# Layer 2's sums of bases in two parts, and copies from DRAM to DRAM beside layer 1's edges

## The chip, the cores and the metric

The kernel runs on one core of one Trainium2 chip. The metric is the device time of one execution in microseconds; a comparison uses the medians of several executions. A core has five engines that matter here: TensorE (PE), VectorE (DVE), ScalarE (ACT), GpSimd (POOL) and SyncE (SP), which only issues transfers. Each works its own instructions in order, and semaphores tie them together.

## What is computed

The reference is two graph layers of one kind, a mixture of experts, four graph layers of another kind and a quantized feed-forward part, each added to a running x of 10000 rows of 512. Only the first piece matters here:

```python
def rgcn_gate_layer(x, row, col, edge_type, basis, att, gate_w, root, bias):
    w = jnp.einsum('rb,bio->rio', att, basis)          # 2 relations, 30 bases of 512 x 512
    x_j = x[col]                                       # 5000 edges
    msgs = []
    for r in range(NUM_RELATIONS):
        gate = jax.nn.sigmoid(x_j @ gate_w[r, :, 0])
        msgs.append(gate[:, None] * x_j @ w[r])
    msg = jnp.where((edge_type == 0)[:, None], msgs[0], msgs[1])
    agg = jax.ops.segment_sum(msg, row, num_segments=x.shape[0])
    return agg + x @ root + bias
...
h = jax.nn.relu(rgcn_gate_layer(x, ..., basis1, att1, ...))
out = rgcn_gate_layer(h, ..., basis2, att2, ...)
...
x = x + _L0_gnn_ref(_layernorm(x, axis=-1), ...)
```

So each of the two layers needs two weighted sums of 30 matrices (one for each relation), a product for every node (`x @ root`), and a gated product for every edge that is added to the row of its target.

## The kernel before

The work runs in stages: the sorting of the edges, the node pass of layer 1, the edges of layer 1, the edges of layer 2, and then the rest (the node product of layer 2, the experts, the other graph layers). DRAM tensors link them: `xn_d` holds the normalized rows, `r1_d` layer 1's sums, and `a2_d` the rows to which layer 2's edges are added.

*Node pass* (`rgcn_nodes1`). It goes over 20 blocks of up to 512 rows. A block is loaded into `x_in`, stored unchanged into `a2_d`, normalized into `xn` and stored into `xn_d`, turned by PE, multiplied with `root` (L742), copied by ACT to `o_nodes` (L746), given the bias by POOL (L748) and stored into `r1_d`. The blocks' loads and stores are all on SP's queue (`rows_to`, L139).

*Sums of bases* (`relation_weights`). For each of 30 bases SP loads 1 MB into one of the two buffers of the pool `stream`, and DVE adds it into the weights of both relations (L635 for the first basis, L637 for the others). A sum works on 128x2048 numbers.

*Edges* (`rgcn_edges`). There are RT = 41 tiles of 128 sorted edges. A tile is gathered from DRAM by POOL (`fetch`, L614). In `make_ready` DVE takes its two dot products with the gate vectors (L669), ACT the sigmoid (L674), DVE the mask of the relation (L675); PE turns the keys (L680), and DVE makes `same` (L682), a matrix that adds up edges with the same target. In `add_up` PE multiplies by it (L689) and ACT copies the result to `aT` (L693). In `put` PE multiplies by the weights (L703), ACT copies to `o` (L708), and POOL adds the rows to DRAM with a scatter (`scatter_add`, L619). The loop runs over i: tile i is fetched, tile i-3 made ready, tile i-5 added up, tile i-6 put. On PE, POOL, ACT and DVE the order of this loop is the one written (`manual_schedule`); everything outside it, and all of SP's queue, is put in order by a scheduler, which lets later work fill the gaps that it sees.

*Placing* (`place_nodes`). A generator of some sixty small steps, which the edges' loops carry beside them: `take(i)` says in which iterations a step is taken. Ten of the steps are `equal_keys`, in which PE turns four columns of keys into a PSUM pool of two buffers and DVE compares each (L211, L212).

In the program's order, layer 1's sums stand behind the node pass; layer 2's sums stand between the two loops of edges, but DVE may take them earlier.

Of the kernel before, what the change touches and what calls it, by code (L numbers as in the profile page):

```python
# [8 lines left out]
F32 = mybir.dt.float32  # L9
# [4 lines left out]
OP = mybir.AluOpType  # L14
# [3 lines left out]
P = 128  # L18
N = 10000
D = 512  # L20
KC = D // P
E = 5000
ET = 40
# [19 lines left out]
CAP = 625  # L43
CT = (CAP + P - 1) // P
LAYERS = 4
FETCHED, READY = 6, 3
LN_EPS = 1e-5
BN_EPS = 1e-5
# [21 lines left out]
def gnn_ffn_kernel(ctx: ExitStack, tc: tile.TileContext, I, out, dram):  # L70
# [62 lines left out]
    def rows_to(sb, d, b, store=False):  # L133

        for n, a0, a1 in block_parts(b):
            r0 = (b * 4 + a0) * P
            v = d[r0 : r0 + n * (a1 - a0), :].rearrange("(a p) d -> p a d", p=n)
            s = sb[:n, a0:a1, :]
            nc.sync.dma_start(v, s) if store else nc.sync.dma_start(s, v)  # L139

    def row_broadcast(pool, d, width, name):

        t = pool.tile([P, width], F32, name=name)
        nc.sync.dma_start(t, bass.AP(tensor=d.tensor, offset=d.offset, ap=[[0, P], [1, width]]))
        return t
# [467 lines left out]
    def gather(dst, src, idx):  # L613
        return nc.gpsimd.indirect_dma_start(  # L614
            out=dst, out_offset=None, in_=src, in_offset=bass.IndirectOffsetOnAxis(ap=idx, axis=0)
        )
# [6 lines left out]


    def relation_weights(basis, att_d, pool, stream, tag):
        att = row_broadcast(pool, att_d, RELATIONS * BASES, f"att_{tag}")
        ws = pool.tile([P, RELATIONS, KC * D], F32, name=f"w_{tag}")
        for b in range(BASES):
            t = stream.tile([P, KC, D], F32, name="basis")
            nc.sync.dma_start(t, basis[b].rearrange("(k p) o -> p k o", p=P))  # L630
            tf = t.rearrange("p k o -> p (k o)")
            for r in range(RELATIONS):
                c = att[:, r * BASES + b : r * BASES + b + 1]
                if b == 0:
                    nc.vector.tensor_scalar(ws[:, r], tf, c, None, op0=OP.mult)  # L635
                else:
                    nc.vector.scalar_tensor_tensor(ws[:, r], tf, c, ws[:, r], op0=OP.mult, op1=OP.add)  # L637
        return ws

    def rgcn_edges(tag, meta, src_d, relu, ws, gate_d, dst_d, beside, take):  # L640

        with ExitStack() as s:
            fix = s.enter_context(tc.tile_pool(name=f"re_fix_{tag}", bufs=1))
            wk = s.enter_context(tc.tile_pool(name=f"re_wk_{tag}", bufs=3))
            pk = s.enter_context(tc.tile_pool(name=f"re_pk_{tag}", bufs=1, space=PSUM))
            pa = s.enter_context(tc.tile_pool(name=f"re_pa_{tag}", bufs=2, space=PSUM))
            po = s.enter_context(tc.tile_pool(name=f"re_po_{tag}", bufs=2, space=PSUM))
            gate = row_broadcast(fix, gate_d, RELATIONS * D, "gate")  # L650
            of_rel = fix.tile([P, RT, RELATIONS], F32, name="of_rel")
            nc.vector.tensor_scalar(of_rel[:, :, 0], meta["attr"], 0.0, None, op0=OP.is_equal)
            nc.vector.tensor_scalar(of_rel[:, :, 1], meta["attr"], 0.0, None, op0=OP.not_equal)
            w_all = ws.rearrange("p r w -> p (r w)")

            got, ready, sums = {}, {}, {}

            def fetch(t):
                got[t] = wk.tile([P, D], F32, name="x", bufs=FETCHED + 2)
                gather(got[t], src_d, meta["gidx"][:, t : t + 1])  # L660

            def make_ready(t):
                x, kt = got[t], meta["key"][:, t : t + 1]
                if relu:
                    nc.scalar.activation(x, x, AF.Relu)
                dots = wk.tile([P, RELATIONS], F32, name="dots")
                prod = wk.tile([P, D], F32, name="prod", bufs=2)
                for r in range(RELATIONS):
                    nc.vector.scalar_tensor_tensor(  # L669
                        prod, x, 1.0, gate[:, r * D : (r + 1) * D], op0=OP.mult, op1=OP.mult,  # L670
                        accum_out=dots[:, r : r + 1],
                    )
                g = wk.tile([P, RELATIONS + 1], F32, name="g")
                nc.scalar.activation(g[:, :RELATIONS], dots, AF.Sigmoid)  # L674
                nc.vector.scalar_tensor_tensor(  # L675
                    dots, g[:, :RELATIONS], 1.0, of_rel[:, t, :], op0=OP.mult, op1=OP.mult,
                    accum_out=g[:, RELATIONS:],
                )
                ps_k = pk.tile([P, P], F32, name="ps_k")
                nc.tensor.transpose(ps_k, kt.to_broadcast([P, P]), ident)  # L680
                same = wk.tile([P, P], F32, name="same", bufs=4)
                nc.vector.tensor_scalar(same, ps_k, kt, g[:, RELATIONS:], op0=OP.is_equal, op1=OP.mult)  # L682
                ready[t] = same

            def add_up(t):
                x, same = got.pop(t), ready.pop(t)
                ps_a = pa.tile([P, KC, P], F32, name="ps_a")
                for k in range(KC):
                    nc.tensor.matmul(  # L689
                        ps_a[:, k, :], lhsT=x[:, k * P : (k + 1) * P], rhs=same, start=True, stop=True  # L690
                    )
                sums[t] = wk.tile([P, KC, P], F32, name="aT")
                nc.scalar.copy(sums[t], ps_a)  # L693

            def put(t):
                aT = sums.pop(t)
                w0 = nc.values_load(
                    meta["w_at"][:, t : t + 1], engines=(mybir.EngineType.PE,), min_val=0, max_val=KC * D,
                    skip_runtime_bounds_check_because="it is 0 or KC * D by the comparison that makes it",
                )  # L700
                ps_o = po.tile([P, D], F32, name="ps_o")
                for k in range(KC):
                    nc.tensor.matmul(  # L703
                        ps_o, lhsT=aT[:, k, :], rhs=w_all[:, bass.ds(w0 + k * D, D)],
                        start=k == 0, stop=k == KC - 1,
                    )
                o = wk.tile([P, D], F32, name="o")
                nc.scalar.copy(o, ps_o)  # L708
                scatter_add(dst_d, meta["sidx"][:, t : t + 1], o)

            E_ = mybir.EngineType
            with tc.manual_schedule(engines={E_.PE, E_.Pool, E_.Activation, E_.DVE}):
                for i in range(RT + FETCHED):
                    if i < RT:
                        fetch(i)
                    if i >= FETCHED - 1 and i - FETCHED + 1 < RT:
                        add_up(i - FETCHED + 1)
                    if i >= FETCHED:
                        put(i - FETCHED)
                    if READY <= i < RT + READY:  # L720
                        make_ready(i - READY)
                    if take(i):
                        next(beside, None)

    def rgcn_nodes1(root, bias, pools):


        ld, tp, small, pt, po = pools
        for b in range(NB):
            tiles, parts, cols = block_tiles(b), block_parts(b), block_cols(b)  # L730
            x = ld.tile([P, 4, D], F32, name="x_in")
            rows_to(x, I["x"], b)
            rows_to(x, a2_d, b, store=True)
            xn = ld.tile([P, 4, D], F32, name="xn")
            layernorm(small, xn, x, tiles, parts, on_act=True)
            rows_to(xn, xn_d, b, store=True)
# [15 lines left out]

    with ExitStack() as s:
        wpool = s.enter_context(tc.tile_pool(name="w_rel", bufs=1))
        stream = s.enter_context(tc.tile_pool(name="stream", bufs=2))
        src_meta = s.enter_context(tc.tile_pool(name="src_meta", bufs=1))
        wk = s.enter_context(tc.tile_pool(name="sort", bufs=1))
        place_wk = s.enter_context(tc.tile_pool(name="place_wk", bufs=1))
# [1 line left out]
        with ExitStack() as n:  # L760
# [18 lines left out]
                meta_pool,  # L779
            )  # L780
            rgcn_nodes1(root, bias, (ld, tp, small, pt, po))
            ws = relation_weights(I["L0_gnn_basis1"], I["L0_gnn_att1"], wpool, stream, "1")
        placing = place_nodes(by_dst, place_wk, ps, meta_pool)
        rgcn_edges(
            "1", by_src, xn_d, False, ws, I["L0_gnn_gate_w1"], r1_d, placing,
            lambda i: i >= FETCHED and i % 2 == 0,
        )
        ws = relation_weights(I["L0_gnn_basis2"], I["L0_gnn_att2"], wpool, stream, "2")
        rgcn_edges("2", by_src, r1_d, True, ws, I["L0_gnn_gate_w2"], a2_d, placing, lambda i: True)
        for _ in placing:  # L790
            pass

# [753 lines left out]
    with ExitStack() as n:  # L1546
# [36 lines left out]
        def fetch(t):  # L1583
            if t < NT:
                n_ = rows_of(t // 4, t % 4)
                old[t] = wk.tile([P, D], F32, name="x_old", bufs=3)
                gather(old[t][:n_], x2_d, node_at[:n_, t : t + 1])
# [233 lines left out]
```

## Time and profile before

| | us |
|---|---|
| median of 3 runs | 4662.56 (4658.36 to 4666.1) |
| the profiled execution | 4666.98 |
| its span | 4665.2 |
| first gather of layer 1's edges | at 532.50 |
| first and last scatter of layer 1's edges | at 565.51 and 839.71 |
| first gather of layer 2's edges | at 845.12 |
| layer 2's sums on DVE | 408.6 to 628 |

Times inside the profile count from the start of the span. A line of a group gives the line of the kernel, the engine, the operation, its output and inputs, and how often it ran. A line of the order of time gives the start, the duration, the engine and the operation, and in brackets how long the engine had been idle before it and what released it. The releaser is inferred from semaphores, and where several were waited for, only one is named.

### The profile page before, as it was taken

What the parts mean: (1) busy time and instruction counts of PE and PEld (TensorE: products, weight loads), DVE (VectorE), ACT (ScalarE), POOL (GpSimd) and SP (SyncE); (2) the same over time, 40 slices, a digit from 0 to 9 for tenths busy, and PEclk for the clock granted to TensorE, in tenths of its full rate; (3) what the DMA queues carried; (4) which work ended last, traced back from release to release, by engine and by line L of the source; (5) the groups of instructions that cost most, each with busy time, mean ns of one, the idle gap of its engine ahead of it and who ended that gap; (6) DMA issues with size and microseconds to landing.
All of it is one profiled execution on the core that took longest, in us unless ns stands there. A gap on an engine that the chain in (4) does not pass through costs nothing.

```text
span 4665.2 us, 42798 instructions
## 1 busy us (share of the span) xinstructions
PE 4046.1 (87%) x13624; PEld 2048.0 (44%) x13624; DVE 2820.7 (60%) x5906; ACT 1679.5 (36%) x2992; POOL 1569.0 (34%) x1127
## 2 busy tenths in 40 slices
PE   6799568897999945968887999999999999999997
PEld 3443234443444422434443555545555455544443
DVE  7887865554545465646755546644575455755776
ACT  4334112232333310116423523354233532334775
POOL 3434334441000036865542113311142111422443
PEclk9899789898988866989889999999999999999998
DMA  8677654457555414986411123102231012311332
GB/s 276 228 260 258 216 123 88 86 105 184 192 171 182 146 48 84 162 164 218 153 54 43 73 77 119 42 17 81 85 108 37 27 75 104 90 30 46 110 109 98
DMA packets 293120, 556.20 MB, mean 119 GB/s; under 512 B 41216, under 2 KB 71969, under 8 KB 291871
## 3 DMA queue, kind: packets, MB, share of 16 engines
q1 hardware_dynamic: 219632, 364.67, 23.2%
q0 software_dynamic: 73264, 188.79, 17.8%
q8 instruction: 111, 1.82, 0.2%
q14 instruction: 113, 0.93, 0.1%
HBM read 292.40 MB, written 260.95 MB: 119 GB/s over the span
## 4 chain that ended last, share of the span: by engine, by line
PE 38%; DVE 8%; DMA 4%; ACT 3%; issue 2%; POOL 1%; POOLq 0%; DVEq 0%; ACTq 0%
PE ps_b L1317 15%; PE ps_d L1317 8%; PE ps_o L1593 5%; PE ps_e L1317 4%; PE ps_x L1424 2%; DMA x<-xg_d,gpos 2%; PE ps_x L1248 2%; ACT feat L1413 1%; DMA x_in<-x_d,node_at 1%; DVE stats L1402 1%; DVE x L1234 1%; DVE feat L1252 1%; PE ps_q L1661 1%; DVE feat L1332 1%; DVE t L1340 0%
## 5 line engine op out<-in xcount | busy, mean ns | idle before, releaser
L1317 PE MATMUL ps_b<-feat,w 128*128 128x512 f32 (+1 forms) x1120 | 499.7, 587 | 25.6 <-ACT feat L1413 25.5
L1317 PE MATMUL ps_d<-feat,w_s 128*128 128x512 f32 (+1 forms) x1120 | 503.6, 586 | 4.3 <-issue 3.1
L1325 ACT ACTIVATE feat<-ps_b,cols 128x512 f32<-128x512 f32 (+1 forms) x300 | 203.8, 683 | 568.1 <-PE ps_b L1317 555.4
L1352 POOL TENSOR_TENSOR feat<-feat 128x1024 f32<-128x1024 f32 (+1 forms) x70 | 162.5, 2322 | 623.2 <-DVE feat L1351 598.2
L1365 POOL TENSOR_TENSOR feat<-feat,p 128x1024 f32<-128x1024 f32 (+1 forms) x70 | 176.3, 2519 | 483.0 <-ACT feat L1325 474.2
L637 DVE SCALAR_TENSOR_TENSOR w<-basis,att,w 128x2048 f32<-128x2048 f32 x116 | 315.8, 2731 | 15.6 <-DMA basis<-in_L_gnn_basis 15.6
L742 PE MATMUL ps_o<-root,xT 128*128 128x512 f32 (+1 forms) x632 | 323.6, 625 | 0.0
L1317 PEld LDWEIGHTS ps_b<-feat,w 128*128 128x128 f32 x1120 | 208.4, 191 | 255.5 <-issue 209.4
L703 PE MATMUL ps_o<-w,aT 128*128 x656 | 304.6, 609 | 0.1
L1426 DVE TENSOR_TENSOR x_rows<-ps_x,be 128x512 f32<-128x512 f32 (+1 forms) x237 | 157.4, 685 | 231.0 <-PE ps_x L1424 231.0
L1317 PEld LDWEIGHTS ps_d<-feat,w_s 128*128 128x128 f32 x1120 | 203.3, 192 | 202.2 <-issue 183.0
L918 PE MATMUL ps_n<-root,rT 128*128 128x512 f32 (+1 forms) x632 | 288.6, 613 | 0.0
L1317 PE MATMUL ps_b<-t,w_s 128*128 128x512 f32 (+1 forms) x560 | 259.2, 603 | 21.7 <-ACT feat L1325 21.6
L1317 PE MATMUL ps_e<-feat,w 128*128 128x512 f32 (+1 forms) x560 | 264.9, 614 | 12.9 <-DVE feat L1283 12.9
L614 POOL DMA_INDIRECT x<-xg_d,gpos x160 | 175.0, 1093 | 287.8 <-issue 71.8
L1317 PE MATMUL ps_b<-feat,w_s 128*128 128x512 f32 (+1 forms) x560 | 253.7, 591 | 0.0
L1413 ACT ACTIVATE feat<-feat,bn_sm 128x512 f32<-128x512 f32 (+2 forms) x320 | 236.6, 809 | 3.4 <-DVE bn_sm L1532 3.4
L1234 DVE SCALAR_TENSOR_TENSOR x<-we,srt_d,x 128x512 f32<-128x512 f32 x160 | 139.9, 889 | 156.6 <-DMA x<-xg_d,gpos 149.5
L1402 DVE BATCH_NORM_STATS2 stats<-feat 128x6 f32<-128x512 f32 (+1 forms) x320 | 202.7, 667 | 46.7 <-POOL feat L1365 33.1
L1248 PE MATMUL ps_x<-same,x 128*128 128x128 f32 x1280 | 176.9, 287 | 58.6 <-DVE same L1244 24.1
L1248 PEld LDWEIGHTS ps_x<-same,x 128*128 128x128 f32 x1280 | 167.9, 199 | 126.9 <-issue 42.2
L1237 ACT ACTIVATE x<-x 128x512 f32<-128x512 f32 x160 | 99.3, 628 | 295.2 <-DVE x L1234 179.3
(483 smaller groups left out, 7656.1 us busy)
## 6 DMA issues: line engine op xcount, KB each, us to landing
basis<-in_L_gnn_basis SPq DMA_DIRECT2D x60, 1024.0 KB
xg_d<-x_rows SPq DMA_DIRECT2D x234, 256.0 KB
xg_d<-x_in SPq DMA_DIRECT2D x39, 512.0 KB
x_in<-in_x SPq DMA_DIRECT2D x19, 1024.0 KB
a_d<-x_in SPq DMA_DIRECT2D x19, 1024.0 KB
xn_d<-xn SPq DMA_DIRECT2D x19, 1024.0 KB
r_d<-o_nodes SPq DMA_DIRECT2D x19, 1024.0 KB
r_in<-r_d SPq DMA_DIRECT2D x19, 1024.0 KB
```

The costliest lines, as they stand in the source:

```text
L637: nc.vector.scalar_tensor_tensor(ws[:, r], tf, c, ws[:, r], op0=OP.mult, op1=OP.add)
L703: nc.tensor.matmul(ps_o, lhsT=aT[:, k, :], rhs=w_all[:, bass.ds(w0 + k * D, D)], start=k == 0, stop=k == KC - 1,)
L742: nc.tensor.matmul(ps_o[:n], lhsT=xT[:, k, a * P : a * P + n], rhs=root[:, k, :], start=k == 0, stop=k == KC - 1,)
L918: nc.tensor.matmul(ps_o[:n_], lhsT=rT[:, k, a * P : a * P + n_], rhs=root[:, k, :], start=k == 0, stop=k == KC - 1,)
L1234: nc.vector.scalar_tensor_tensor(x, we, by_dst["attr"][:, t : t + 1], x, op0=OP.mult, op1=OP.add)
L1248: nc.tensor.matmul(ps_a[:, k, :], lhsT=x[:, k * P : (k + 1) * P], rhs=same, start=True, stop=True)
L1317: nc.tensor.matmul(ps[fo], lhsT=A[a][:, k, fo * P : (fo + 1) * P], rhs=x[:, k, :], start=first and k == 0, stop=k == 1, skip_group_check=True,
L1325: nc.scalar.activation(dst[:, fo, :], ps[fo], func, bias=b, scale=scale)
L1365: nc.gpsimd.tensor_tensor(b22, b22, p5, OP.add)
L1402: nc.vector.bn_stats(stats[:, k, 2 * p + j, :], big[:, k, s0 + j * w : s0 + (j + 1) * w])
L1413: nc.scalar.activation(hb, hb, AF.Relu, bias=sm[:, fo, 3:4], scale=sm[:, fo, 2:3])
L1593: nc.tensor.matmul(ps_o[:n_], lhsT=big[:, kc, t * P : t * P + n_], rhs=W2[kc], start=kc == 0, stop=kc == KC - 1,)
```

## The change

Four things change.

1. `relation_weights` no longer runs its sums at once. It returns the weights' tile and a generator that adds one basis at each step. Layer 1's are all taken at once, as before. Of layer 2's, eight (`EARLY_BASES`) are taken inside the node stage, behind layer 1's; the other 22 are taken one by one inside layer 1's loop of edges, at i = 4, 6, ... 46, on DVE behind `make_ready`.
2. Placing steps in layer 1's loop are taken at odd i from 7 on; before it was even i from 6 on. In layer 2's loop each iteration takes one, as before.
3. The node pass no longer stores its rows into `a2_d`. Instead, in each of the first 40 iterations of layer 1's loop, SP issues a copy of 250 rows from the input x to `a2_d`, from DRAM to DRAM. The copy of iteration i waits until that iteration's gather has landed.
4. The pool `stream` has three buffers instead of two.

```diff
+EARLY_BASES = 8
...
     def relation_weights(basis, att_d, pool, stream, tag):
...
-        for b in range(BASES):
...
-        return ws
+        def sums():
+            for b in range(BASES):
+                t = stream.tile([P, KC, D], F32, name="basis")
+                nc.sync.dma_start(t, basis[b].rearrange("(k p) o -> p k o", p=P))
+                tf = t.rearrange("p k o -> p (k o)")
+                for r in range(RELATIONS):
+                    c = att[:, r * BASES + b : r * BASES + b + 1]
+                    if b == 0:
+                        nc.vector.tensor_scalar(ws[:, r], tf, c, None, op0=OP.mult)
+                    else:
+                        nc.vector.scalar_tensor_tensor(ws[:, r], tf, c, ws[:, r], op0=OP.mult, op1=OP.add)
+                yield
+
+        return ws, sums()
...
                     if i < RT:
-                        fetch(i)
+                        fetched = fetch(i)
...
-                    if take(i):
-                        next(beside, None)
+                    beside(i, fetched)
...
             rows_to(x, I["x"], b)
-            rows_to(x, a2_d, b, store=True)
...
-        stream = s.enter_context(tc.tile_pool(name="stream", bufs=2))
+        stream = s.enter_context(tc.tile_pool(name="stream", bufs=3))
...
             rgcn_nodes1(root, bias, (ld, tp, small, pt, po))
-            ws = relation_weights(I["L0_gnn_basis1"], I["L0_gnn_att1"], wpool, stream, "1")
+            ws1, adding = relation_weights(I["L0_gnn_basis1"], I["L0_gnn_att1"], wpool, stream, "1")
+            for _ in adding:
+                pass
+            ws2, adding = relation_weights(I["L0_gnn_basis2"], I["L0_gnn_att2"], wpool, stream, "2")
+            for _ in range(EARLY_BASES):
+                next(adding)
         placing = place_nodes(by_dst, place_wk, ps, meta_pool)
+
+        def beside_1(i, ready):
+            if i >= 4 and i % 2 == 0:
+                next(adding, None)
+            elif i > FETCHED:
+                next(placing, None)
+            if i < ET:
+
+                c0, c1 = N * i // ET, N * (i + 1) // ET
+                cp = nc.sync.dma_start(a2_d[c0:c1, :], I["x"][c0:c1, :])
+                tc.add_manual_dep(
+                    cp.ins, ready.ins.name,
+                    mybir.DependencyInfo(mybir.DependencyClass.Sync, mybir.DependencyReason.DATA),
+                    reason="not all at once, and not beside the nodes",
+                )
+
+        rgcn_edges("1", by_src, xn_d, False, ws1, I["L0_gnn_gate_w1"], r1_d, beside_1)
+        for _ in adding:
+            pass
         rgcn_edges(
-            "1", by_src, xn_d, False, ws, I["L0_gnn_gate_w1"], r1_d, placing,
-            lambda i: i >= FETCHED and i % 2 == 0,
+            "2", by_src, r1_d, True, ws2, I["L0_gnn_gate_w2"], a2_d, lambda i, _: next(placing, None)
         )
-        ws = relation_weights(I["L0_gnn_basis2"], I["L0_gnn_att2"], wpool, stream, "2")
-        rgcn_edges("2", by_src, r1_d, True, ws, I["L0_gnn_gate_w2"], a2_d, placing, lambda i: True)
```

More of the change, by code (lines that the diff above doesn't have):

```diff
@@ L627, in relation_weights, with rgcn_edges @@
         ws = pool.tile([P, RELATIONS, KC * D], F32, name=f"w_{tag}")
-        for b in range(BASES):
[L629 to L637, printed above, removed]
-        return ws
-    def rgcn_edges(tag, meta, src_d, relu, ws, gate_d, dst_d, beside, take):
+        def sums():
[11 more added lines that the diff above has]
+        return ws, sums()
+    def rgcn_edges(tag, meta, src_d, relu, ws, gate_d, dst_d, beside):
         with ExitStack() as s:
@@ L659, in fetch @@
                 got[t] = wk.tile([P, D], F32, name="x", bufs=FETCHED + 2)
-                gather(got[t], src_d, meta["gidx"][:, t : t + 1])
+                return gather(got[t], src_d, meta["gidx"][:, t : t + 1])
             def make_ready(t):
```

## The prediction

> **What bounds the kernel now.** I read the page first (span, engine shares, groups), then the busy time by stage, then POOL's and SP's order of time where the stage of the change begins, then DVE's order of time inside it, and last the DMA view of two windows.
>
> ```profile
> span 4665.2 us, 42798 instructions
> ...
> L637 DVE SCALAR_TENSOR_TENSOR w<-basis,att,w 128x2048 f32<-128x2048 f32 x116 | 315.8, 2731 | 15.6 <-DMA basis<-in_L_gnn_basis 15.6
> ```
>
> A sum takes 2.73 us on average, 2.34 in the median; a basis has two.
>
> ```profile
> 250.00:500.00 250.00, 238.82 (x745) 100.53 (x745) 204.12 (x388) 100.24 (x213) 106.68 (x52) 0.98 0.72 246
> 500.00:640.00 140.00, 53.52 (x163) 28.16 (x163) 118.31 (x135) 12.68 (x28) 43.26 (x22) 0.68 0.66 198
> 640.00:800.00 160.00, 137.01 (x519) 75.83 (x518) 74.73 (x309) 35.68 (x84) 74.83 (x56) 0.98 0.52 92
> ```
>
> Columns: stretch, its length, busy time of PE, PE loads, DVE, ACT, POOL, clock, DMA share, GB/s. The node pass (to 500) has PE busy 238.8 of 250 us. From 500 to 640 PE idles, 53.5 of 140, and DVE is full, 118.3: that is the hole. After 640 PE is the fullest again and DVE is under half.
>
> ```profile
> 504.88 12.51 SPq L630 DMA_DIRECT2D basis<-in_L_gnn_basis  x3
> ...
> 522.18 1.21 SPq L139 DMA_DIRECT2D r_d<-o_nodes  x2
> ```
> ```profile
> 507.14 7.70 POOL L748 TENSOR_TENSOR o_nodes<-o_nodes,bias 128x1024 f32<-128x1024 f32 x2 [4.43 <-ACT o_nodes L746]
> 532.50 3.14 POOL L614 DMA_INDIRECT x<-xn_d,gidx_s  x1 [17.66 <-DVE w L637]
> ...
> 565.51 2.00 POOL L619 DMA_INDIRECT r_d<-o,sidx  x1 [20.74 <-ACT o L708]
> 567.82 2.24 POOL L614 DMA_INDIRECT x<-xn_d,gidx_s  x1 [0.30 <-issue]
> 572.38 3.51 POOL L619 DMA_INDIRECT r_d<-o,sidx  x1 [2.32 <-DVE dots L675]
> ...
> 834.20 1.55 POOL L619 DMA_INDIRECT r_d<-o,sidx  x1 [3.93 <-issue]
> 839.71 1.55 POOL L619 DMA_INDIRECT r_d<-o,sidx  x1 [3.95 <-DMA r_d<-o,sidx]
> 845.12 1.01 POOL L614 DMA_INDIRECT x<-r_d,gidx_s  x1 [3.86 <-DMA r_d<-o,sidx]
> ```
>
> Three things to see. POOL ends the last bias add at 514.84, but SP issues the last node stores at 522.18 to 523.39, because loads of bases that wait for DVE stand ahead of them; the first gather goes out at 532.50. (Its named releaser is a sum of DVE; the last stores landing fits too, and since both go in the change I need not choose.) The scatters run from 565.51 to 839.71: 40 intervals, 6.86 us each; the first five take 72.4 us, the other 35 take 5.77 each. And at the end, with nothing else to wait for, each scatter still waits 3.95 us for the one before to land: 1.55 + 3.95 = 5.50 us a tile is the floor of this chain.
>
> ```profile
> 642.23 0.16 DVE L675 SCALAR_TENSOR_TENSOR dots<-g,of_rel 128x2 f32<-128x2 f32 x1 [2.41 <-ACT g L674]
> ...
> 649.18 0.16 DVE L675 SCALAR_TENSOR_TENSOR dots<-g,of_rel 128x2 f32<-128x2 f32 x1 [3.25 <-ACT g L674]
> ```
> ```profile
> q0 software_dynamic: 2434, 5.69, 55.2%
> ```
> ```profile
> q1 hardware_dynamic: 5469, 10.87, 58.4%
> ```
>
> DVE idles 2.41 + 3.25 = 5.66 us in each pair of tiles (11.39 us). The two queue lines are of 640 to 700 (gathers and scatters alone) and of 560 to 620 (bases too): packets, MB, share of 16 engines.
>
> **The change, part by part.** The sum is against the profiled execution, 4666.98 us (span 4665.2 and 1.8 around it), 4.4 above the median 4662.56.
>
> *Before the first gather.* Today 15 of layer 2's bases are summed by 541, the eighth at about 488; then DVE goes on without a pause, and SP's loads wait for it. With only eight ahead, DVE is quiet from about 488 and SP's stores wait for nobody. ACT's last copy to o_nodes ends at 510.5; a bias add on 16 rows should need about 1.3 us when no sum runs beside it (3.3 now), so the stores go out at about 512, and land in 6 us (9.1 now, with bases in flight): first gather at 518, 14 us earlier. Bounds: 0 (another releaser) to 17.
>
> *From gather to first scatter.* Today 33.0 us. The first gather's issue falls from 3.14 us (a sum beside it) to about 1, and the sums of 541 to 565 that stand between the DVE steps fall away but for one basis at i=4, 4.7 us. First product 6.5 us after the gather, `same` 3.3 later, matmuls, copies and the one basis 10.5: 20 us, so the first scatter is at 538.
>
> *The 40 intervals.* Three floors, all near each other:
> (a) PE and DVE. Two sums (4.7 us) now stand on DVE after `same` of each even i; the next `same` comes 7.1 us later (0.32 + 4.62 + two products 1.31 + sigmoid and masks 0.85) instead of 4.43. In odd i stand the placing steps, whose third transpose on PE waits for DVE's first `eq`: the whole delay of 2.7 us lands on PE. A pair costs 11.39 + 2.7 = 14.1 us in the ten `equal_keys` steps; the nine pairs behind them, 11.6 today, get about 13.2, the first one 10.4: 270 us, 6.75 a tile.
> (b) The scatter chain: 1.59 of issue, some 0.4 for issues beside a sum (3.51 at 572.38 against 1.55), and the landing. That is 3.95 alone and at most 4.87 with bases in flight (567.51 to 572.38); with 4.6, 6.6 a tile.
> (c) DMA. From the queue lines: gathers and scatters take 0.552 x 60 us for 10.5 tiles, 3.14 us a tile; a basis 0.584 x 60 us for 10.4 MB-sized loads, 3.38, half of one a tile 1.69. A copy of 250 rows (0.51 MB) is the unknown. At a load's rate it is 1.65 us: 6.5 a tile. If reading and writing DRAM cost a pass each, 3.3: 8.1.
>
> [...] I take 6.5 to 7.2, nearest to the row, since each copy is released by a gather landing, about when the scatter before it has landed, so part of it lies in the gap in which POOL issues.
>
> Three floors at 6.5 to 7.2 don't overlap perfectly: 7.15 a tile, 286 us, last scatter at 824 against 839.7: 16 us earlier.
>
> *Moved past queues.* SP issues 40 copies of about 0.4 us each, 16 us over 290. A copy that waits for a gather holds up the basis loads behind it; with three buffers, a load has about five tiles of lead over its sum, so nothing waits. If that cover were gone, each of 19 loads would show up to 3.4 us on DVE. POOL gets no new instruction.
>
> *Costed at nothing.* The a2 stores and their 21 waits on SP leave the node pass (20.5 MB, 61 us of all engines at a load's rate): PE, 95% busy from 250 to 500, covers it; the bounds are -10 (the 15 us wait for `key_s` before 206 shrinks) to +5 (another order of instructions). The last basis is summed at i=46, when layer 2's first product still waits for gathers; the last copy belongs to i=39, some 40 us ahead of the first scatter into a2_d. Layer 2 itself keeps its length: one placing step more, in a loop that has slots to spare.
>
> Sum: 4667.0 - 16 = 4651, or 4646.6 by the median; I say 4646.
>
> **The rivals.**
> *Slower: DMA becomes the bound.* [...] It decides from (839.7 - 538) / 40 = 7.54 us a tile. For it: the floor is 6.5 even at the kindest price, and layer 1's gathers and scatters alone hold 55% of the engines. Against: with bases in flight a landing stayed under 4.9.
> *Faster by more.* PE's waits for `eq` don't add up because PE has caught up elsewhere, and the copies fit in the gaps: 6.3 a tile, last scatter at 790, 50 us earlier: 4613. For it: the chain's own floor is 5.5, and DVE has 5.66 us idle a pair for 4.7 of sums. Against: floor (c).
> *Nothing to see.* The earlier start is worth 14 + 13 us (first gather, and 20 us instead of 33 to the first scatter). At 7.5 us a tile, 40 x (7.5 - 6.86) = 26 us of it are given back: 4662, within 9. That the change does not do what it says (the scheduler floating sums up into the gaps again) belongs here; inside the hand-written order, though, DVE keeps the written place.
>
> **How the numbers follow.** Forecast 0.5 (4625 to 4660, a fifth of it within 0.2%, some 9 us, which is about what a measurement of this kernel can tell), slower rival 0.25, faster one 0.15, nothing 0.10. Faster 0.4 + 0.15 = 0.55; same 0.1 + 0.1 = 0.20; slower 0.25. The range runs from 4608 to 4692: it leaves out about half of each outer rival.
>
> **What would show it.** First gather near 518, and no sum between 490 and that; first scatter near 538; scatters 7 us apart, last one near 824; odd tiles longer than even ones by 5 us or more, with PE waiting on `eq`; landing after a scatter's issue 4.6 us. DMA share in that stage near 0.9. I am wrong if scatters stand over 7.5 us apart, if POOL's waits there name the scatter before, or if the node pass ends more than 10 us away from 510.

## The result and the profile after

The changed kernel is slower: 4672.16 us (median of 14 runs, 4661.32 to 4690.96) against 4656.73 for the kernel before (14 runs beside it), a ratio of 1.0033 with an interval of 1.0022 to 1.0043. The forecast was 4646 and faster.

The two profiled executions are nearly equal, 4667.41 us after and 4666.98 before; the one of before lies 10 us above the median of its runs, the one of after 5 us below. So the spans say nothing here, and I read the marks of the stage instead (a tile is the distance from the first to the last scatter, divided by 40):

| us from the start of the span | before | forecast | after |
|---|---|---|---|
| first gather | 532.50 | 518 | 517.18 |
| first scatter | 565.51 | 538 | 534.09 |
| a tile (40 intervals) | 6.86 | 7.15 | 7.97 |
| last scatter | 839.71 | 824 | 852.70 |
| first gather of layer 2 | 845.12 | – | 858.06 |
| last scatter of layer 2 | 1094.61 | – | 1102.82 |

Layer 1's edges begin 31.4 us earlier and end 13.0 later. The medians differ by 15.4.

From the page of the changed kernel, its span and the group of the sums:

```profile
span 4665.6 us, 42847 instructions
...
L641 DVE SCALAR_TENSOR_TENSOR w<-basis,att,w 128x2048 f32<-128x2048 f32 x116 | 291.3, 2527 | 14.4 <-DMA basis<-in_L_gnn_basis 14.4
```

The sums became cheaper by themselves, 291.3 us against 315.8 for the same 116. Their own length is not what costs. The busy time by stage (stretch, length, PE, PE loads, DVE, ACT, POOL, clock, DMA share, GB/s):

```profile
250.00:500.00 250.00, 236.47 (x757) 101.10 (x756) 160.57 (x396) 96.88 (x207) 89.03 (x51) 0.97 0.55 186
500.00:640.00 140.00, 96.69 (x316) 53.50 (x316) 80.57 (x195) 24.32 (x55) 60.52 (x38) 0.83 0.66 188
640.00:800.00 160.00, 111.79 (x361) 62.16 (x361) 96.77 (x227) 25.93 (x59) 60.12 (x41) 0.82 0.72 193
450.00:500.00 50.00, 49.42 (x148) 22.30 (x147) 4.61 (x27) 16.96 (x34) 16.22 (x9) 1.00 0.39 120
```

The hole of 500 to 640 is half filled, PE 96.7 us against 53.5. But the stage behind it, which was good before, has become like it: PE 111.8 of 160 instead of 137.0, at a clock of 0.82 instead of 0.98. No engine is full there, and DMA is busy for 72%. The last row shows what I had not expected: DVE works 4.61 us in the 50 us ahead of the hole. The eight bases were done at 398.

POOL's order of time:

```profile
513.27 1.25 POOL L751 TENSOR_TENSOR o_nodes<-o_nodes,bias 16x512 f32<-16x512 f32 x1 [1.13 <-ACT o_nodes L749]
517.18 1.01 POOL L615 DMA_INDIRECT x<-xn_d,gidx_s  x1 [2.65 <-issue]
...
534.09 1.64 POOL L620 DMA_INDIRECT r_d<-o,sidx  x1 [8.07 <-ACT o L714]
...
637.36 1.58 POOL L620 DMA_INDIRECT r_d<-o,sidx  x1 [2.92 <-DVE prod L675]
...
647.21 1.58 POOL L620 DMA_INDIRECT r_d<-o,sidx  x1 [6.97 <-ACT g L680]
...
652.94 1.58 POOL L620 DMA_INDIRECT r_d<-o,sidx  x1 [2.06 <-DVE prod L675]
...
838.69 4.15 POOL L620 DMA_INDIRECT r_d<-o,sidx  x1 [4.14 <-DMA r_d<-o,sidx]
846.78 1.90 POOL L620 DMA_INDIRECT r_d<-o,sidx  x1 [3.94 <-issue]
852.70 1.55 POOL L620 DMA_INDIRECT r_d<-o,sidx  x1 [4.02 <-DMA r_d<-o,sidx]
858.06 1.01 POOL L615 DMA_INDIRECT x<-r_d,gidx_s  x1 [3.80 <-DMA r_d<-o,sidx]
```

The bias add takes 1.25 us and the gather follows at 517.18: the start went as forecast. A long and a short interval make a pair: 9.85 and 5.73 us here, 15.6 in all, where 14.1 was forecast (and a difference of 5 or more, for 4.1 here). The issue of 4.15 us at 838.69 is a scatter beside a sum. Inside the long interval, in PE's order of time with one sum of DVE:

```profile
638.52 0.95 PE L212 MATMUL ps_s<-ident,key_d 128*128 128x128 f32 x2 [3.92 <-DVE eq L213]
...
639.26 1.91 PE L695 MATMUL ps_a<-same,x 128*128 128x128 f32 x8
...
640.97 5.29 PE L709 MATMUL ps_o<-w,aT 128*128 x8
...
646.21 1.06 PE L695 MATMUL ps_a<-same,x 128*128 128x128 f32 x8
...
647.10 3.60 PE L709 MATMUL ps_o<-w,aT 128*128 x8
...
647.67 4.61 DVE L641 SCALAR_TENSOR_TENSOR w<-basis,att,w 128x2048 f32<-128x2048 f32 x2
...
655.00 0.95 PE L212 MATMUL ps_s<-ident,key_d 128*128 128x128 f32 x2 [3.98 <-DVE eq L213]
```

PE waits 3.92 us for `eq`, which stands on DVE behind the sums. Then the same eight products that take 1.06 us in the next tile take 1.91, and the eight behind them 5.29 instead of 3.60: another 2.5 us. This is the clock, as the busy time of these two tiles shows (the granted clock is the third number from the end):

```profile
639.26:646.21 6.95, 6.95 (x19) 3.88 (x18) 1.81 (x8) 0.58 (x1) 0.98 (x1) 0.63 0.99 299
646.21:650.65 4.44, 4.44 (x20) 2.47 (x19) 3.48 (x5) 1.27 (x3) 3.14 (x2) 1.00 0.67 141
```

It repeats behind each of the ten waits: there the first eight products take 1.91 or 1.92 us, and the granted clock over both groups is 0.61 to 0.79, against 1.00 in the tiles between.

The waits in the stage from 530 to 850 (engine, output, line, what it waited for: us in all, times, longest), and the two DMA queues from 640 to 700 (packets, MB, share of 16 engines):

```profile
PE ps_s L212 <- DVE eq L213: 46.5, 10, 7.7
...
PE ps_s L458 <- DVE tot_f L456: 14.7, 1, 14.7
...
DVE w L641 <- DMA basis<-in_L_gnn_basis: 14.4, 6, 5.6
```
```profile
q1 hardware_dynamic: 2353, 7.81, 41.4%
q0 software_dynamic: 1709, 3.96, 31.4%
```

The ten `equal_keys` steps wait 46.5 us; the placing steps behind them have long single waits. Gathers and scatters take 31.4% of the engines instead of 55.2%, in part because fewer tiles pass (3.96 MB instead of 5.69).

### The profile page after: what moved, and what is told of

It reads as the page before. It is cut to its first block, busy times and chain, and to the rows that moved or that the text cites. A ratio compares the mean times of both kernels' runs of the same rounds, so it can differ in the third digit from the quotient of the medians.

```text
span 4665.6 us, 42847 instructions
## 1 busy us (share of the span) xinstructions
PE 4065.5 (87%) x13624; PEld 2062.4 (44%) x13624; DVE 2809.1 (60%) x5906; ACT 1681.2 (36%) x2992; POOL 1555.4 (33%) x1127
## 4 chain that ended last, share of the span: by engine, by line
PE 37%; DVE 9%; DMA 4%; ACT 3%; issue 2%; POOL 1%; DVEq 0%; POOLq 0%; ACTq 0%
PE ps_b L1341 14%; PE ps_d L1341 8%; PE ps_o L1617 5%; PE ps_e L1341 4%; PE ps_x L1448 2%; DMA x<-xg_d,gpos 2%; PE ps_x L1272 2%; DVE stats L1426 1%; ACT feat L1437 1%; DMA x_in<-x_d,node_at 1%; DVE feat L1276 1%; DVE x L1258 1%; PE ps_q L1685 1%; DVE feat L1356 1%; DVE t L1364 1%
## 5 line engine op out<-in xcount | busy, mean ns | idle before, releaser
L641 DVE SCALAR_TENSOR_TENSOR w<-basis,att,w 128x2048 f32<-128x2048 f32 x116 | 291.3, 2527 | 14.4 <-DMA basis<-in_L_gnn_basis 14.4
```

## The experiments

Medians; the ratio is to the kernel before, run beside each. First and last scatter come from the profiled execution, and "a tile" is their distance over 40. Executions of these kernels spread by 12 to 48 us, so a single profile tells where time is spent, and the ratio what it is worth.

| run | us | ratio | first, last scatter | a tile |
|---|---|---|---|---|
| after | 4672.16 | 1.0033 [1.0022, 1.0043] | 534.1, 852.7 | 7.97 |
| e1 placing, then sums | 4674.94 | 1.0052 [1.0035, 1.0069] | 536.3, 852.3 | 7.90 |
| e2 no copies | 4666.31 | 1.0021 [1.0008, 1.0034] | 537.8, 841.2 | 7.59 |
| e3 copies alone | 4685.66 | 1.0070 [1.0049, 1.0090] | 579.3, 847.4 | 6.70 |
| e4 all 30 ahead | 4634.79 | 0.9957 [0.9942, 0.9972] | 573.2, 833.3 | 6.50 |
| e5 e1 without copies | 4653.55 | 1.0006 [0.9997, 1.0016] | 544.2, 839.9 | 7.39 |
| e6 e5, 20 ahead | 4628.01 | 0.9950 [0.9934, 0.9967] | 574.8, 819.4 | 6.11 |
| e7 30 ahead, no copies | 4657.98 | 1.0017 [1.0006, 1.0028] | 618.2, 847.9 | 5.74 |
| e8 e1 without loads | 4617.9 (one run) | – | 530.5, 811.1 | 7.02 |
| e9 20 ahead | 4647.8 | 0.9969 [0.9957, 0.9981] | 540.8, 825.2 | 7.11 |
| e10 halves | 4665.96 | 1.0011 [0.9997, 1.0025] | 531.6, 838.8 | 7.68 |
| e11 halves, no copies | 4631.11 | 0.9942 [0.9928, 0.9956] | 546.1, 816.6 | 6.76 |
| e12 e10, older gather | 4654.69 | 0.9987 [0.9974, 0.9999] | 543.3, 861.1 | 7.94 |
| e13 e11, 14 ahead | 4641.76 | 0.9962 [0.9953, 0.9972] | 567.4, 821.1 | 6.34 |
| e14 e12, four buffers for o | 4643.21 | 0.9982 [0.9971, 0.9993] | 538.5, 832.6 | 7.35 |

### Sums or copies: each alone, and the order on DVE (e1 to e4)

e1 takes the placing step in even iterations, ahead of the sums, so that `eq` no longer stands behind them:

```diff
         def beside_1(i, ready):
+            if i >= FETCHED and i % 2 == 0:
+                next(placing, None)
             if i >= 4 and i % 2 == 0:
                 next(adding, None)
-            elif i > FETCHED:
-                next(placing, None)
```

> In layer 1's loop the placing step and the two sums both stand in the even iterations, the placing step first. The work and the transfers are those of the changed kernel. If PE's wait for eq behind the two sums (3.98 us at 655.00) and the slow matmuls after it are the cost (theory A), a pair of tiles falls from 16.0 to about 12 us, the last scatter comes near 534 + 40 x 6.1 = 778, and the kernel takes about 4600. If the transfers beside the loop cost it (B), or DVE's plain load (C), the pair stays at 15 to 16 us and the time within 10 us of the changed kernel's 4672.

PE's wait for `eq` fell, but nothing was gained: 7.90 a tile. Its waits from 530 to 850, then SP's and DVE's order of time:

```profile
DVE w L641 <- DMA basis<-in_L_gnn_basis: 67.4, 14, 7.1
...
PE ps_k L686 <- DVE same L688: 48.3, 13, 8.4
...
PE ps_s L212 <- DVE eq L213: 17.8, 15, 2.1
```
```profile
613.54 8.75 SPq L801 DMA_DIRECT2D a_d<-in_x  x2
622.38 0.53 SPq L634 DMA_DIRECT2D basis<-in_L_gnn_basis  x1
...
631.03 4.61 DVE L641 SCALAR_TENSOR_TENSOR w<-basis,att,w 128x2048 f32<-128x2048 f32 x2 [6.70 <-DMA basis<-in_L_gnn_basis]
```

Two copies hold SP's queue from 613.54 to 622.29, while they wait for their gathers; the load of a basis behind them goes out at 622.38, and DVE, whose sum needs it, waits 6.70 us and starts at 631.03. Nothing else runs on DVE in these 6.70 us. So a second bound stood right behind the first.

e2 leaves out the copies and stores the rows in the node pass again (`rows_to(x, a2_d, b, store=True)`, as before):

```diff
+            rows_to(x, a2_d, b, store=True)
...
-            if i < ET:
...
-                cp = nc.sync.dma_start(a2_d[c0:c1, :], I["x"][c0:c1, :])
...
```

> The sums as in the changed kernel, but no copies from DRAM to DRAM: the rows are stored into a2_d in the node pass as before. A: pairs still 15.5 to 16 us, last scatter 850, the time of the changed kernel within 10 us. B: with 20 MB less beside the loop, pairs fall to 14 or less, last scatter before 820, at least 30 us faster than the changed kernel.

Still slower than before. PE's order of time is that of the changed kernel:

```profile
653.37 0.95 PE L212 MATMUL ps_s<-ident,key_d 128*128 128x128 f32 x2 [3.93 <-DVE eq L213]
...
654.11 1.91 PE L695 MATMUL ps_a<-same,x 128*128 128x128 f32 x8
```

So, in these two profiled executions, the sums alone, as this change places them, make 7.59 of the 7.97 us, and the copies the last 0.38.

e3 is the kernel before with the copies in place of the a2 stores; the text of the sums stays as it was:

```diff
                     if i < RT:
-                        fetch(i)
+                        fetched = fetch(i)
...
+                    if tag == "1" and i < ET:
+                        c0, c1 = N * i // ET, N * (i + 1) // ET
+                        cp = nc.sync.dma_start(a2_d[c0:c1, :], I["x"][c0:c1, :])
...
-            rows_to(x, a2_d, b, store=True)
```

> The kernel before, with the copies from DRAM to DRAM beside layer 1's edges in place of the stores in the node pass; sums and placing as before. A: scatters beyond the hole stay 5.8 to 6.3 us apart (the copies cost at most 0.5 a tile), the kernel is within 15 us of the one before. B: 7 us apart or more, 40 us slower than before.

The dearest of all, but not by the copies alone: the sums went elsewhere. SP's and DVE's order of time:

```profile
557.63 241.03 SPq L726 DMA_DIRECT2D a_d<-in_x  x40
...
857.46 9.13 DVE L637 SCALAR_TENSOR_TENSOR w<-basis,att,w 128x2048 f32<-128x2048 f32 x4
```

The 40 copies, which wait for their gathers, hold SP's queue from 557.63 to 798.66, and the loads of the last six bases stand behind them. So no sum runs between 569 and 830, and a tile still takes 6.70 us, against 5.77 in the kernel before behind its first five intervals. The last six bases are added from 830.70 on, most of them among layer 2's first tiles: its first scatter comes 38.7 us after its first gather instead of 20.3, and its edges take 264 us against 249. So this run does not give the price of the copies by itself; e7 below does.

e4 is the changed kernel with no sum in the loop:

```diff
-EARLY_BASES = 8
+EARLY_BASES = 30
```

> EARLY_BASES = 30: all of layer 2's sums ahead of layer 1's edges, none among them; copies and odd placing steps as in the changed kernel. DVE sits idle from 398 to about 523 in the changed kernel, 22 bases of 4.7 us need 103. A and C: scatters 5.8 to 6.2 us apart from the first on, the first one at 534 to 550, the last near 780, and the time 60 to 75 us under the changed kernel's, so also under the one before: 4600 to 4610. B: the copies still hold the loop at 7 us a tile or more, last scatter past 815.

Faster than before, with 6.50 a tile. The first gather went out at 538.11, and its issue took 19 us where the next takes 0.96:

```profile
512.32 43.92 DVE L641 SCALAR_TENSOR_TENSOR w<-basis,att,w 128x2048 f32<-128x2048 f32 x18
...
538.11 19.01 POOL L615 DMA_INDIRECT x<-xn_d,gidx_s  x1 [17.96 <-DMA r_d<-o_nodes]
557.43 0.96 POOL L615 DMA_INDIRECT x<-xn_d,gidx_s  x1 [0.30 <-issue]
```

It ends at 557.12, 0.9 us after the last of 18 sums that run back to back: the issue began among them and went on past their end.

### What holds the loop without the first cause (e5 to e8)

e5 has both edits, e1's and e2's.

> Both edits of the first two experiments together: the placing step and then the two sums in the even iterations, and no copies beside the loop (rows stored into a2_d in the node pass). In the first experiment DVE waited 67 us for bases whose loads stood on SP behind copies that wait for gathers. Theory D (two limits of the same size, one behind the other: PE waiting on a late DVE, and loads late behind copies): with both gone a pair takes 12 us or less, last scatter near 538 + 40 x 6 = 778, and the kernel 4595 to 4610. If DVE's plain load is the limit (C), the pair stays above 14 us and the time above 4645.

A miss: the pairs stayed at 14.7 us. PE's waits for `eq` are mostly short and no sum waits for a load, but `same` of each even tile is late, behind ACT. Its waits, and PE's order of time after a short wait:

```profile
ACT o L714 <- DMA r_d<-o,sidx: 75.5, 16, 7.7
...
PE ps_s L212 <- DVE eq L213: 24.6, 14, 4.8
```
```profile
646.23 0.32 PE L212 MATMUL ps_s<-ident,key_d 128*128 128x128 f32 x1 [2.03 <-DVE eq L213]
...
646.86 1.07 PE L695 MATMUL ps_a<-same,x 128*128 128x128 f32 x8
```

After a wait of 2.03 us the eight products take 1.07 us and the next eight 3.60, no longer than in a tile without a wait, unlike after 3.9. But in e11 waits of 1.67 us were followed, from 600 to 680, by groups of 1.07 to 1.87 and then by groups of 3.69 to 5.34, at a mean granted clock of 0.90 (600 to 700). So each of the ten waits of the changed kernel, 3.9 us and longer, had slower products behind it, and so had most of those of 1.67 us in e11; a length under which none has them the runs don't show.

e6 is e5 with `EARLY_BASES = 20`.

> As the one before, with EARLY_BASES = 20, so ten bases among the edges. DVE's idle time from 398 to 517 holds about 20 bases, so the first gather should still go out near 518 to 525. D: scatters 5.8 us apart, last one near 540 + 40 x 5.85 = 774, 4590 to 4605, the best of all. C: 12 bases less in the loop, so half of the gain from 7.6 to 5.8 us a tile: 4625.

It is one of the two fastest of the timed versions, 0.5% ahead of the kernel before: 30 us of late start (first scatter at 574.8) bought 1.3 us a tile.

e7 is e4 without the copies, in e2's way.

> All 30 bases ahead, no copies beside the loop (stores in the node pass). Against the run with all ahead and copies, whose scatters were 6.5 us apart: if the copies stretch the landing of each scatter, the distance falls to 5.6 to 5.8 us, the first scatter stays near 573, the last comes near 803, 30 us earlier, and the time 4605 to 4615. If the copies cost nothing, 6.4 us apart and within 10 us of 4635.

5.74 a tile against 6.50 in e4: the copies' price in a loop without sums is 0.76 a tile, 30 us. But the first scatter moved from 573 to 618: with the a2 stores back in the node pass the sums come late, and the first gather's issue took 21.83 us. The whole is 0.6% dearer than e4. So the copies pay in one place and cost in the other.

e8 is e1 with the sums in the loop taking the last loaded basis again, without loads:

```diff
-                t = stream.tile([P, KC, D], F32, name="basis")
-                nc.sync.dma_start(t, basis[b].rearrange("(k p) o -> p k o", p=P))
+                if tag == "1" or b < EARLY_BASES:
+                    t = stream.tile([P, KC, D], F32, name="basis")
+                    nc.sync.dma_start(t, basis[b].rearrange("(k p) o -> p k o", p=P))
```

> The first experiment (placing step, then sums, copies kept), where the sums inside the loop add the last basis loaded again and no basis is loaded there; layer 2's weights are thus other numbers. If the late loads behind the copies held that run (D), DVE's wait for bases is gone and the scatters stand 6.4 to 6.6 us apart, the price of the copies alone, last one near 536 + 262 = 798. If copies and DVE's load together did, still over 7.4.

With the copies but without loads e1's loop goes from 7.90 to 7.02. It is one execution, and takes the loads' traffic away with their lateness.

### More ahead, and shorter sums (e9 to e11)

e9 is the changed kernel with `EARLY_BASES = 20`, nothing else.

> The changed kernel with one number altered: 20 bases ahead of layer 1's edges, 10 among them; the copies stay. Theory F (a basis in the loop costs about 2 us more than a basis in the hole saves; the eight ahead leave DVE idle for some 100 us in front of the loop): first scatter some 15 to 25 us later than 534, that is at 550 to 560; the first 20 intervals at 8 us, the other 20 at 6.5 as in the run with all 30 ahead: 160 + 130 = 290 us, last scatter at 840 to 848; the whole 4654 to 4664. Rival G (the number ahead hardly matters once copies run beside the loop, since DMA carries the same bytes either way): within 5 us of the changed kernel.

24 us faster than the changed kernel by the medians, and faster than before. Twelve more bases delayed the first scatter by only 7 us, less than expected, since DVE was idle there. Had they been free in the loop, nothing would have been won; they cost (7.97 - 7.11) x 40 = 34 us there, 2.9 us each.

e10 cuts a step of the generator in two, one relation after each `make_ready`:

```diff
                         nc.vector.scalar_tensor_tensor(ws[:, r], tf, c, ws[:, r], op0=OP.mult, op1=OP.add)
-                yield
+                    yield
...
-            for _ in range(EARLY_BASES):
+            for _ in range(RELATIONS * EARLY_BASES):
...
-            if i >= 4 and i % 2 == 0:
-                next(adding, None)
-            elif i > FETCHED:
+            if i > FETCHED and i % 2:
                 next(placing, None)
+            if i >= 3:
+                next(adding, None)
```

> The changed kernel with its sums cut in two: one relation of a basis behind make_ready of every tile (from i = 3 on) instead of both relations behind every second one; placing steps stay at odd i, ahead of the sum. Same work, same loads, same copies; DVE is closed for 2.3 us at a time instead of 4.6. Theory A (it is the closed stretch of 4.6 us that PE's third transpose waits for, after which TensorE runs at a lower clock): PE's waits for eq fall under 15 us in all and the loop goes to 7.2 to 7.5 us a tile, last scatter at about 825 to 835, the whole 4648 to 4658. Rival H (what counts is the total of DVE's sums beside the loop, through POOL's slowed issues and the loads behind SP's copies): 7.8 to 8.0 a tile as before, the whole within 5 us of the changed kernel.

Between the two: 7.68 a tile. As in e1, the loads came late:

```profile
DVE w L641 <- DMA basis<-in_L_gnn_basis: 65.0, 15, 7.6
...
PE ps_s L212 <- DVE eq L213: 32.8, 14, 4.3
```

e11 is e10 without the copies.

> As the run with halved sums, without the copies (the rows are stored into a2_d in the node pass again). Theory A: with neither the closed stretch of 4.6 us nor copies, the loop falls under 7 us a tile, to 6.4 to 6.9; first scatter at about 540 as in the earlier runs without copies, last at 800 to 815; the whole 4628 to 4642. Rival H: 7.4 to 7.6 a tile, the whole 4653 to 4666.

Theory A came out to the numbers: 6.76 a tile, 4631. Against e2 the only edit is the cut of the sum in two, one half behind each `make_ready`, and the ratio falls from 1.0021 to 0.9942. The stretch from 650 to 750, first in e2, then in e11, has PE at 71.7 and at 83.3 of 100 us, DVE at 65 and at 76, and the clock at 0.82 and at 0.90:

```profile
650.00:750.00 100.00, 71.70 (x232) 41.23 (x233) 64.95 (x165) 16.57 (x38) 41.09 (x27) 0.82 0.57 145
650.00:750.00 100.00, 83.25 (x287) 45.37 (x286) 75.99 (x187) 20.88 (x48) 45.25 (x30) 0.90 0.63 156
```

The sums are the same in number and length in both runs, so without copies neither DVE's total work nor POOL's slower issues made the loop slow; the closed stretch of 4.6 us did. Beside the copies the same cut gained only 0.2% (after to e10), with intervals that overlap.

### Queue or traffic (e12 to e14)

e12 lets each copy of e10 wait for an older gather:

```diff
             if i < ET:
+                landed.append(ready)
+                ready = landed[max(0, i - 4)]
```

> As the run with halved sums and copies, but the copy of iteration i waits for the gather of tile i - 4 instead of its own; the copies, their bytes and their order stay. Theory J (the copies cost by their place on SP's queue: a copy that waits 7 us for its gather holds the load of a basis behind it, and its sum then waits on DVE): the copies issue at once, DVE's waits for basis loads fall from 65 us to under 20, and the loop goes from 7.68 to 6.9 to 7.3 us a tile; the whole 4635 to 4652. Rival K (the copies cost by their traffic: landings of gathers, scatters and loads are stretched): waits for loads stay above 45 us or turn into waits for landings, 7.5 to 7.8 a tile, the whole 4660 to 4672.

No sum waits for a load any more. The median gained 0.24% on e10, about 11 us, the ratios' intervals just overlapping; without copies (e11) it is another 0.45%, 21 us, with the a2 stores back in the node pass. The profiled execution was the slowest of the 22, so its 7.94 a tile stands for itself alone. The place on SP's queue thus seems to be a third of what the copies cost beside halved sums; the rest is not settled by this run.

e13 is e11 with `EARLY_BASES = 14`.

> Halved sums without copies, and 14 bases ahead instead of eight; 16 in the loop, over by i = 34. Theory F (what eight leave undone in the hole is paid in the loop at more than it costs in the hole): first scatter at most 5 us later than with eight (546 to 551), 32 intervals at 6.7 and eight at 5.7, last scatter at 806 to 814: the whole 4622 to 4630. Rival: sums in front of the first gather hold up the node pass's stores and POOL's first issues as in the run with twenty ahead (first scatter 575): the whole 4630 to 4640.

The rival was right: the first gather moved from 526.99 to 547.89, the loop's gain (6.34) did not make up for it, and the median is 11 us above e11, the ratios' intervals just overlapping.

e14 gives `o` four buffers in e12:

```diff
-                o = wk.tile([P, D], F32, name="o")
+                o = wk.tile([P, D], F32, name="o", bufs=4)
```

> As the run whose copies wait for older gathers, with four buffers for o instead of three. Theory L (ACT waits for a buffer of o, so a late landing goes on through ACT's sigmoid to DVE's mask and PE's transposes): ACT's waits for a landing fall from 97.8 us to under 15, the loop to 7.0 to 7.4 us a tile, the whole 4630 to 4645. Rival M (a landing only ends at the same time as PE's product, and is named by chance; what holds the loop is PE behind eq at a lower clock): the same kernel within 5 us, some 4650 to 4660, and the waits go to another name.

0.9982 against 0.9987, intervals overlapping almost wholly: a fourth buffer brought nothing that can be told. ACT's waits that name a landing fell to 37.9 us, but in a quicker execution. What holds the loop beside copies when loads and `eq` come in time stays open.

## Why the prediction was wrong

**The start: right.** First gather at 517.18 for 518, first scatter at 534.09 for 538.

**Eight bases done at 488: wrong.** They were done at 398. In e2, where the a2 stores are still in the node pass, the last of them ends at 484.6. I had asked what leaving out the stores does to PE, and answered nothing; I had not asked what it does to the loads on the same queue. Without the stores the sums ended some 85 us earlier. (The stores' 20.5 MB are 66 us of all engines at the rate of the loads, not 61; nothing hangs on it.) DVE then had little to do for 100 us ahead of the hole, and 22 bases were left for the loop. e9 shows what this was worth: 24 us.

**Floor (a), 6.75 us a tile: the step that failed first.** The wait was there as described, on the third transpose, ten times, and the delay was about right. In the kernel before, PE waits 1.49 us there:

```profile
643.24 0.32 PE L211 MATMUL ps_s<-ident,key_d 128*128 128x128 f32 x1 [1.49 <-DVE eq L212]
...
643.87 1.07 PE L689 MATMUL ps_a<-same,x 128*128 128x128 f32 x8
```

Now it waits 3.92, 2.4 us more for 2.7 forecast. But this delay was all that I had added. What the longer wait does to PE's clock I had put at nothing: behind 1.49 us the eight products take 1.07, behind 3.92 they take 1.91, and the pair shown loses another 2.5 us. From one wait to the next (638.52 to 655.00) PE's pair takes 16.5 us. The 11.4 of before, 2.4 of longer wait and 2.5 of slower products are nearly all of it; I had 14.1. The nine pairs behind the `equal_keys` steps, which I gave 13.2, took 15.6 (the last 18 intervals); their placing steps have single waits of up to 14.7 and 9.4 us. Without the copies the loop takes 7.59 (e2), and with the closed stretch halved 6.76 (e11).

**Floor (b), 6.6: about right as a floor, and not the bound.** The landing was some 4.1 to 4.5 us (5.7 to 6.1 from the start of the issue, in the DMA view, less 1.58 of issue) for 4.6; POOL's waits name the scatter before in 8 cases, 32.5 us, against 71.9 in which they name ACT's `g`. Beside sums an issue took up to 4.15 us, for which 0.4 on the average was allowed.

**Floor (c), 6.5 to 7.2: the lower price was right, the meaning was not.** In e4's DMA view from 600 to 740 the copies are alone on their queue:

```profile
q1 hardware_dynamic: 688, 11.27, 25.7%
```

11.27 MB are 22 copies of 0.51 MB, and 25.7% of 140 us is 36.0 us, 1.64 each, 313 GB/s: about a load's rate, which the line of q1 in the prediction gives as 310 (10.87 MB in 58.4% of 60 us). No run shows the 7.2 a tile at the upper end: with the copy at 1.64 the prediction's own sum of DMA is 3.14 + 1.69 + 1.64 = 6.5. In e4's view a copy has some 31 packets (688 for 22 copies), and 360 packets of all are of 8 KB or more, some 16 a copy. The DMA share in the changed kernel is 0.72, not 0.9: DMA did not bound by its sum. The copies cost by stretching the chain, 0.76 us a tile with no sums there (e4 against e7).

**"Five tiles of lead, so nothing waits": wrong.** A copy waits for a gather at the head of SP's queue, and the load behind it comes after its sum is due: 14.4 us of waits in the changed kernel, 67.4 in e1 and 65.0 in e10, once the longer wait is gone.

**Layer 2 and the node pass: right within some us.** The last bias add ends at 514.52, for 514.84 before; layer 2's edges take 244.8 us against 249.5.

**The sum.** 40 x (7.97 - 7.15) = 32.8, less 3.9 for the earlier first scatter, is 28.9: the last scatter at 853 for 824. The break-even of 7.54 was right, and of what I named as signs of being wrong the first came true. The slower rival had the direction, but not the cause: it wanted a DMA that is full, and the share was 0.72 from 640 to 800.

The error as a whole was to take floors that lie close together for nearly independent and to add 0.4 us to the highest. Each cause hid the other: taking away the closed stretch alone gains 0.2% (e10), the copies alone 0.1% (e2), both by intervals that overlap with the changed kernel's, and the two together 0.9% (e11). The third buffer of `stream` was not tried by itself.

## What to carry to other kernels

Work put into the gaps of an engine cost here by its longest closed piece, not by its sum: ask what of another engine stands behind it in the same iteration, and cut it so that the piece fits into that slack (e2 to e11, one edit, 35 us by the medians). When traffic is taken out of a stage, ask what on the same queue moves forward, and fit the split of the work to the new times. A DMA that waited on an event at the head of a queue was a wait for the loads behind it (67.4 us of DVE's waits in e1, six bases held to the end of the loop and past it in e3); a lead counted in buffers, three in e1, didn't help there.

## What the hardware showed

GpSimd's issue of an indirect gather took 19.01 us beside 18 of VectorE's sums that ran back to back (e4), and the first one took 21.83 us in e7 and 8.36 in e6; with no sum beside it, it took 1.01 (the changed kernel, at 517.18) and 0.96 (e4's next). A scatter's issue took 4.15 us beside a sum in the changed kernel (at 838.69), against 1.55 with none (before, at 839.71); the longest in e5's loop took 5.92.

In the changed kernel TensorE's products ran at about half the speed after waits of 3.9 us and longer (1.91 or 1.92 against 1.06 us for eight), and more slowly in the next group as well (3.88 to 5.55 against 3.60). In the pair shown (from 639.26) the granted clock was 0.63 over both groups, and the wait of 3.9 us cost 6.4.

A copy of 250 rows from DRAM to DRAM ran at about a load's rate, 1.64 us of all engines (e4, 600 to 740).
